# A graph-transformer layer: the linear attention's projections moved out of the sorting stage into the gather stage

## Chip, core and metric

The kernel runs on one core of a Trainium2 chip. A core has a matrix engine (TensorE, PE in the profile), a vector engine (VectorE, DVE), a scalar engine for activation functions (ScalarE, ACT), a general engine (GpSimd, POOL) and a sequencer that issues transfers (SyncE, SP). They run side by side and wait for each other by semaphores. [...] The metric is device time in microseconds of one execution, lower is better.

## What is computed

One layer of a graph transformer over 6,250 nodes with 256 features and 206,250 directed edges. Three parts, added up: graph attention over the edges, linear attention over all nodes, and a mixture of eight experts, of which two are chosen per node.

```
xn = layernorm(x)                                  # 6250 x 256
# graph attention: per edge (i <- j), 4 heads
p = xn @ W; e = exp(leaky_relu(p_i . Wl + p_j . Wr))
gnn_i = elu(sum_j e_ij * p_j / sum_j e_ij + b)
# linear attention, 4 heads of 32
q, k, v = split(rmsnorm(xn, g_pre) @ w_qkv)        # 128 columns each
k, v = concat(memory columns, k), concat(memory columns, v)
q = softmax over a head's 32 columns, times 32**-0.5
k = softmax over all nodes
context = k.T @ v                                  # per head, 32 x 32
mix = rmsnorm(q @ context @ w_out + b_out, g_out) + xn
x = x + gnn + mix
x = x + moe(layernorm(x)[None])                    # 8 experts, gelu, top 2
```

The softmax of k runs over all nodes, so its sum and its maximum for each of the 128 columns are only known when every node has been seen; q needs the context and so comes after.

## The kernel before

The nodes are cut into 49 tiles of 128 (the last has 106 rows), in 13 groups of up to four. The kernel has two stages of unlike work and a tail.

**The first stage** sorts the edges and makes the table from which they are gathered. The edges lie in 51 batches of 32 columns. `sort_batch` (L370) handles one: VectorE marks each edge's bucket (`ob`, L387), TensorE counts them (`n_ps`, L395), VectorE scans the counts (`inc`, L399) and spreads them (`ahead`, L412), TensorE forms ranks (`r_ps`, L419 and L420), VectorE takes their maximum (`rank`, L427), ScalarE converts it (`rank2`, L439), VectorE builds the payload (`rv`, two at L444) and the one-hot places (`ohp`, L448), TensorE puts the payload in place (`g_ps`, L454) and ScalarE stores it in `grid` (L459). The tiles `ob`, `inc`, `rank2`, `rv` and `ohp` have two buffers, `r_ps`, `n_ps` and `g_ps` one.

Between the batches `project` (L303) takes one group of nodes for every three batches: statistics on ScalarE, the normalized rows `xn` (L338), two transposes (L343), their copy `xT` (L345), and one product with a joined weight `wcat` (L348) whose 456 columns hold q, k, v (384) and what the graph part needs (72). ScalarE copies q to `q_all` (L351), k and v to `kv` (L352) and the rest to `tab` (L355), which goes to the table in memory. The scale of the rmsnorm, `rn`, is made per group by VectorE (L325 to L328), and the gain `g_pre` is multiplied into the weights once (L291).

When the last group is done, `context` (L467) runs between the remaining twelve batches: VectorE takes the maximum of k over all nodes (L468), GpSimd subtracts it (L498), ScalarE takes the exponential (L499), and TensorE adds up 49 products of k and v in one PSUM region (L502). The result, normalized and multiplied with `w_out`, is `cw` (L521).

**The gather stage** goes through the 49 tiles. `pack` (L875) prepares the edge lists of two tiles, in seven steps of products (`s_ps`, L940) with VectorE's operands (L923, L930, L935). `gather` (L969) lets GpSimd issue 35 indirect transfers per tile into `xe` (L972); `xe` has three buffers. `look` (L980) finds the destination terms (`oh` L984, transposes L997, `ohT` L1001, `e_ps` L1009), `weights` (L1016) makes the edge weights, and `sums` (L1035) adds up the weighted rows in four parts per tile (`ohw` L1041, `a_ps` L1048). A buffer of `xe` comes free when the tile's products at L1048 are done.

Beside the tiles runs a list of other work, `todo` (L1056), from which `some_more` (L1058) takes steps, each at a cost: a call takes up to two units (FC is 2), and a tile has four calls. First on it is `attention` (L574), three steps per group, priced at 2 each: softmax of q (L583 to L588); per tile a transpose, a product with `cw` (L598) and a square sum (L601); the normalization, with x read again (L609), added and written to `base_y` (L620). Its first VectorE operations are held behind the first finished pack by `later` (L567). When it is used up, the experts' weights are loaded and `finish_steps` (L661) of the finished blocks follows: products at L775 and L791, activation at L783, the sum at L795.

**The tail** finishes the experts of the last blocks.

The order on each engine is set by a scheduler at build time; each engine then runs its own list strictly in order. The prices at L1056 fix between which tiles a step stands.

Of the kernel before, what the change touches and what calls it, by code (L numbers as in the profile page):

```python
# [1 line left out]

# [6 lines left out]
F32 = mybir.dt.float32  # L9
F16 = mybir.dt.float16  # L10
BF16 = mybir.dt.bfloat16
I32 = mybir.dt.int32
AF = mybir.ActivationFunctionType
OP = mybir.AluOpType
# [3 lines left out]
P = 128  # L18
# [17 lines left out]
def tile_gps_layer(  # L36
# [53 lines left out]
    KW = 2 * HID + 1  # L90
    O_TAB = 3 * HID
    O_EL = O_TAB + H + FO
    PW = O_EL + H
    assert NPAD > N and PW <= 512 and last > 0
# [141 lines left out]
    with tc.tile_pool(name="ids", bufs=1) as lp:  # L236
# [21 lines left out]
    nc.scalar.dma_start(out=wcat[:, :, :3 * HID], in_=w_qkv.rearrange("(c p) f -> p c f", p=P))  # L258
    nc.scalar.dma_start(
        out=wcat[:, :, O_TAB + H:O_EL], in_=gnn_W.rearrange("(c p) f -> p c f", p=P)  # L260
    )
# [3 lines left out]
    gpre = kp.tile([P, DC], F32, name="gpre")  # L265
# [5 lines left out]
    wo = kp.tile([P, D], F32, name="wo")  # L271
    nc.scalar.dma_start(out=wo, in_=w_out)
    mk = kp.tile([P, NM], F32, name="mk")
    nc.scalar.dma_start(out=mk, in_=mem_kv[0].rearrange("h d m -> (h d) m"))
    mv = kp.tile([P, NM], F32, name="mv")
# [6 lines left out]
    for c in range(DC):  # L282
        wt_ps = mps.tile([FO, P], F32, name="tp")
        nc.tensor.transpose(wt_ps, wcat[:, c, O_TAB + H:O_EL], ident)
        wT = qw.tile([FO, P], F32, name="wT")
        nc.scalar.copy(wT, wt_ps)
        wlr_ps = mps.tile([P, 2 * H], F32, name="pr")
        nc.tensor.matmul(wlr_ps, lhsT=wT, rhs=lrT, start=True, stop=True)
        nc.scalar.copy(wcat[:, c, O_TAB:O_TAB + H], wlr_ps[:, :H])
        nc.scalar.copy(wcat[:, c, O_EL:PW], wlr_ps[:, H:])  # L290
        nc.vector.tensor_scalar(  # L291
            wcat[:, c, :3 * HID], wcat[:, c, :3 * HID], gpre[:, c:c + 1], None, op0=OP.mult
        )

    q_all = qp.tile([P, NT, HID], F32, name="q_all")
    kv = kp.tile([P, NT, KW], F32, name="kv")
    nc.gpsimd.memset(kv[:, :, KW - 1:KW], 1.0)
    kmax = kp.tile([P, HID], F32, name="kmax")

    def xn_of():  # L300
        return qw.tile([P, D], F32, name="xn")

    def project(t0, n):  # L303
# [10 lines left out]
        for j in range(n):  # L314
# [8 lines left out]
        rn = qw.tile([P, GT], F32, name="rn")  # L323
        nc.scalar.activation(rn[:, :n], var, AF.Sqrt, scale=float(D))
        nc.vector.tensor_mul(rn[:, :n], rn[:, :n], rs)  # L325
        nc.vector.tensor_scalar_max(rn[:, :n], rn[:, :n], 1e-12)
        nc.vector.reciprocal(rn[:, :n], rn[:, :n])
        nc.vector.tensor_scalar_mul(rn[:, :n], rn[:, :n], float(D) ** 0.5)  # L328
        shift = qw.tile([P, GT], F32, name="shift")
        nc.vector.scalar_tensor_tensor(  # L330
            shift[:, :n], stats[:, t0:t0 + n, 0], -1.0, rs, op0=OP.mult, op1=OP.mult
# [3 lines left out]
        for j in range(n):  # L335
            t = t0 + j
            xn = xn_of()
            nc.scalar.activation(  # L338
                xn, xt[:, j, :], AF.Identity, bias=shift[:, j:j + 1], scale=rstd[:, t:t + 1]
            )  # L340
            xT_ps = mps.tile([P, DC, P], F32, name="tp")
            for c in range(DC):
                nc.tensor.transpose(xT_ps[:, c, :], xn[:, c * P:(c + 1) * P], ident)  # L343
            xT = qw.tile([P, DC, P], F32, name="xT")
            nc.scalar.copy(xT, xT_ps)  # L345
            pr = mps.tile([P, PW], F32, name="pr")
            for c in range(DC):
                nc.tensor.matmul(  # L348
                    pr, lhsT=xT[:, c, :], rhs=wcat[:, c, :], start=(c == 0), stop=(c == DC - 1)
                )  # L350
            nc.scalar.activation(q_all[:, t, :], pr[:, :HID], AF.Copy, scale=rn[:, j:j + 1])  # L351
            nc.scalar.activation(  # L352
                kv[:, t, :2 * HID], pr[:, HID:3 * HID], AF.Copy, scale=rn[:, j:j + 1]
            )
            nc.scalar.copy(tab[:, j, :], pr[:, O_TAB:PW])  # L355
# [10 lines left out]
    def flat(t):  # L366
        return t.rearrange("p a b -> p (a b)")


    def sort_batch(t):  # L370
# [44 lines left out]
        r_ps = sps.tile([P, BW // BB, 512], F32, name="r_ps")  # L415
# [26 lines left out]
        rv = sw.tile([P, BW, 2, NB], F16, name="rv")  # L442
# [4 lines left out]
        ohp = sw.tile([P, BW, P], F16, name="ohp")  # L447
# [17 lines left out]


    def context():  # L467
        nc.vector.tensor_reduce(  # L468
            kmax, kv[:, :NT - 1, :HID].rearrange("p t d -> p d t"), axis=AX.X, op=OP.max
        )  # L470
        nc.vector.tensor_max(kmax[:last], kmax[:last], kv[:last, NT - 1, :HID])
        km_ps = mps.tile([HID, P], F32, name="tp")
        nc.tensor.transpose(km_ps, kmax, ident)
        kcol = kp.tile([P, 2], F32, name="kcol")
        nc.vector.tensor_reduce(kcol[:, 0:1], km_ps, axis=AX.X, op=OP.max)
        nc.vector.tensor_reduce(kcol[:, 1:2], mk, axis=AX.X, op=OP.max)
        kmc = kp.tile([P, 1], F32, name="kmc")
        nc.vector.tensor_max(kmc, kcol[:, 0:1], kcol[:, 1:2])
        kr_ps = mps.tile([P, HID], F32, name="tp")
        nc.tensor.transpose(kr_ps, kmc.to_broadcast([P, P]), ident)  # L480
        krow = kp.tile([P, HID], F32, name="krow")
        nc.vector.tensor_copy(krow, kr_ps)
        nkm = kp.tile([P, 1], F32, name="nkm")
        nc.vector.tensor_scalar_mul(nkm, kmc, -1.0)
        emk = kp.tile([P, NM], F32, name="emk")
        nc.scalar.activation(emk, mk, AF.Exp, bias=nkm)
        mm_ps = mps.tile([NM, 2, P], F32, name="tp")
        nc.tensor.transpose(mm_ps[:, 0, :], emk, ident)
        nc.tensor.transpose(mm_ps[:, 1, :], mv, ident)
        memT = kp.tile([NM, 2, P + 1], F32, name="memT")  # L490
        nc.vector.memset(memT, 1.0)
        nc.vector.tensor_copy(memT[:, :, :P], mm_ps)
        ctx_ps = mps.tile([P, HID + 1], F32, name="pr")
        nc.tensor.matmul(ctx_ps, lhsT=memT[:, 0, :P], rhs=memT[:, 1, :], start=True, stop=False)
        yield
        for t0, n in groups:
            kk = kv[:, t0:t0 + n, :HID]
            nc.gpsimd.tensor_sub(kk, kk, krow[:, None, :].to_broadcast([P, n, HID]))  # L498
            nc.scalar.activation(kk, kk, AF.Exp)  # L499
            for t in range(t0, t0 + n):  # L500
                rows = P if t < NT - 1 else last
                nc.tensor.matmul(  # L502
                    ctx_ps, lhsT=kv[:rows, t, :HID], rhs=kv[:rows, t, HID:KW],
                    start=False, stop=(t == NT - 1),
                )
            yield
        rden = kp.tile([P, 1], F32, name="rden")
        nc.vector.reciprocal(rden, ctx_ps[:, HID:HID + 1])
        nc.vector.tensor_scalar_mul(rden, rden, float(DH) ** -0.5)
        cbd = kp.tile([P, HID], F32, name="cbd")  # L510
        nc.vector.memset(cbd, 0.0)
        for h in range(MH):
            s = slice(h * DH, (h + 1) * DH)
            nc.vector.tensor_scalar(cbd[s, s], ctx_ps[s, s], rden[s], None, op0=OP.mult)
        cT_ps = mps.tile([P, HID], F32, name="tp")
        nc.tensor.transpose(cT_ps, cbd, ident)
        cT = kp.tile([P, HID], F32, name="cT")
        nc.scalar.copy(cT, cT_ps)
        cw_ps = mps.tile([P, D], F32, name="pr")
        nc.tensor.matmul(cw_ps, lhsT=cT, rhs=wo, start=True, stop=True)  # L520
        nc.scalar.copy(cw, cw_ps)  # L521
        yield
# [21 lines left out]
    steps = context()  # L544
    while batches:
        sort_batch(batches.pop(0))
        next(steps, None)
    for _ in steps:
        pass
# [17 lines left out]
    def later(ins):  # L567

        tc.add_manual_dep(
            ins.ins, gate[0].ins.name,  # L570
            mybir.DependencyInfo(mybir.DependencyClass.NoSync, mybir.DependencyReason.DATA),
        )

    def attention():  # L574
# [4 lines left out]
        for t0, n in groups:  # L579
# [10 lines left out]
            o_g = qw.tile([P, GT, D], F32, name="o_g")  # L590
            ss = qw.tile([P, GT], F32, name="ss")
            for j in range(n):
                qT_ps = yps.tile([P, P], F32, name="y_ps")
                nc.tensor.transpose(qT_ps, q_all[:, t0 + j, :], ident)
                qT = qw.tile([P, P], F32, name="qT")
                nc.scalar.copy(qT, qT_ps)
                o_ps = yps.tile([P, D], F32, name="y_ps")
                nc.tensor.matmul(o_ps, lhsT=qT, rhs=cw, start=True, stop=True)  # L598
                nc.vector.tensor_add(o_g[:, j, :], o_ps, brow)
                sq = qw.tile([P, D], F32, name="sq")  # L600
                nc.scalar.activation(sq, o_g[:, j, :], AF.Square, accum_out=ss[:, j:j + 1])  # L601
# [454 lines left out]
    todo = [(attention(), [FC] * (3 * len(groups)))]  # L1056
# [207 lines left out]
```

## Time and profile before

| | us |
|---|---|
| median of 3 runs (lowest, highest) | 4222.5 (4214.7, 4229.85) |
| the profiled execution | 4182.5 |
| its span, first to last instruction | 4180.7 |
| TensorE busy in the span | 2268.6 (54%) |
| VectorE busy | 1919.8 (46%) |
| GpSimd busy | 1669.8 (40%) |
| ScalarE busy | 746.2 (18%) |
| first gather starts | 446.2 |
| last gather ends | 3994.5 |

Busy time is the time in which an engine works on at least one instruction; a matrix engine's instructions overlap and their ends are modelled. `PEld` is the load of a stationary operand, which runs beside the products. The clock that the throttle granted to TensorE is given as a share of full speed. A wait is put down to whoever released it, by semaphore events; "remote" stands where the profile knows no releaser. The profiled execution was shorter than the median run, by 40 us.

### The profile page before, as it was taken

The numbers are of one execution on the slowest core, as the hardware profiler recorded it, in microseconds if no ns is written. First come the engines' busy times: TensorE is split into PE (matmuls) and PEld (weight loads), VectorE is DVE, ScalarE is ACT, GpSimd is POOL, SyncE is SP. The second block draws the span as 40 slices with busy tenths as digits, with TensorE's granted clock in tenths as the row PEclk, the third lists the DMA queues.
The fourth block names the chain that finished last, engine by engine and source line by source line (L and its number), as shares of the span: only waits on it lengthen the run. The fifth ranks groups of instructions, "written<-read, shape, count | busy, mean of one in ns | idle before, by whom it ended". The sixth has DMA issues, their size and how long they took to land. (4 is left out here: it accounts for less than half of the span.)

```text
span 4180.7 us, 39357 instructions
## 1 busy us (share of the span) xinstructions
PE 2268.6 (54%) x15401; PEld 1663.9 (40%) x15401; DVE 1919.8 (46%) x3941; ACT 746.2 (18%) x1653; POOL 1669.8 (40%) x1774
## 2 busy tenths in 40 slices
PE   7877232435254764644765555455364573554677
PEld 4544232324242543433543433334253352442456
DVE  7787444536352443533442523425343452342423
ACT  5542001212111111111111110111111111110122
POOL 1001545454445344344344344544535335344410
PEclk8875555666666877776877776777676686776778
DMA  1020111111121111011011100101101001011100
GB/s 59 28 29 1 21 28 41 37 41 37 34 74 20 22 19 23 18 24 22 12 29 18 25 17 17 30 17 22 25 12 27 18 19 25 13 25 19 23 12 7
DMA packets 106548, 103.75 MB, mean 25 GB/s; under 512 B 42678, under 2 KB 78740, under 8 KB 106356
## 3 DMA queue, kind: packets, MB, share of 16 engines
q0 software_dynamic: 54720, 60.52, 8.4%
q1 hardware_dynamic: 49940, 39.75, 3.3%
q8 instruction: 123, 2.02, 0.2%
q10 hardware_dynamic: 1696, 0.89, 0.1%
q14 instruction: 69, 0.57, 0.0%
HBM read 86.39 MB, written 14.65 MB: 24 GB/s over the span
## 5 line engine op out<-in xcount | busy, mean ns | idle before, releaser
L972 POOL DMA_INDIRECT xe<-table,dst_x x1710 | 1635.7, 957 | 2011.0 <-PE a_ps L1048 1323.2
L1048 PE MATMUL a_ps<-ohw,xe 128*65 128x128 f32 x4400 | 665.1, 307 | 235.7 <-issue 189.3
L1048 PEld LDWEIGHTS a_ps<-ohw,xe 128*65 128x65 f32 x4400 | 590.8, 159 | 314.4 <-issue 243.1
L775 PE MATMUL h_ps<-tokT,w1s 128*128 128x512 f32 (+3 forms) x896 | 442.8, 610 | 235.1 <-ACT hT L783 205.1
L795 DVE SCALAR_TENSOR_TENSOR x<-y_ps,comb,x 128x256 f32<-128x256 f32 x392 | 187.0, 481 | 782.4 <-remote 479.1
L791 PE MATMUL y_ps<-w2s,hT 128*128 128x256 f32 x1568 | 436.7, 413 | 147.6 <-issue 107.2
L791 PEld LDWEIGHTS y_ps<-w2s,hT 128*128 128x128 f32 x1568 | 315.5, 208 | 273.0 <-issue 177.5
L940 PE MATMUL s_ps<-rc,ohp 128*128 128x144 f16 x2525 | 255.1, 260 | 279.5 <-DVE ohp L935 146.8
L1041 DVE TENSOR_TENSOR ohw<-oh,bank 128x1280 f32<-128x1280 bf16 x196 | 321.5, 1641 | 170.1 <-remote 149.3
L940 PEld LDWEIGHTS <-ohp 128*128 128x128 f16 x2525 | 209.6, 114 | 324.2 <-DVE ohp L935 162.9
L1009 PE MATMUL e_ps<-elw,ohT 128*128 128x48 bf16 x588 | 36.2, 199 | 544.7 <-ACT ohT L1001 477.8
L783 ACT ACTIVATE hT<-h_ps,b1s 128x512 f32<-128x512 f32 (+3 forms) x224 | 140.4, 627 | 1018.4 <-remote 531.0
L775 PEld LDWEIGHTS h_ps<-tokT,w1s 128*128 128x128 f32 x896 | 171.8, 214 | 345.7 <-ACT hT L783 226.0
L1001 ACT COPY ohT<-t_ps 128x768 bf16<-128x768 bf16 x98 | 78.3, 799 | 1130.1 <-remote 842.3
L930 DVE TENSOR_TENSOR rc<-ohc,bank 128x1152 f16<-128x1152 f16 (+1 forms) x350 | 231.2, 687 | 64.8 <-remote 62.2
L1009 PEld LDWEIGHTS <-ohT 128*128 128x128 bf16 x588 | 27.0, 106 | 577.2 <-ACT ohT L1001 505.9
L935 DVE TENSOR_TENSOR ohp<-to,bank 128x2048 f16<-128x2048 f16 (+1 forms) x175 | 193.5, 1105 | 0.0
L763 PE MATMUL y_ps<-b2s,cTs 8*128 8x256 f32 x98 | 49.7, 600 | 192.4 <-ACT cTs L761 118.6
L764 DVE TENSOR_TENSOR x<-x,y_ps 128x256 f32<-128x256 f32 x49 | 20.6, 420 | 269.7 <-remote 164.6
L1018 DVE TENSOR_REDUCE z<-e_ps 128x140 f32<-128x420 f32 (+1 forms) x49 | 28.7, 585 | 244.6 <-PE e_ps L1009 224.1
L923 DVE TENSOR_TENSOR ohc<-to,bank 128x1152 f16<-128x1152 f16 (+1 forms) x175 | 119.6, 683 | 0.3 <-ACT to L911 0.2
L448 DVE TENSOR_TENSOR ohp<-rank,iota_h 128x4096 f16<-128x4096 f16 (+1 forms) x51 | 116.1, 2277 | 6.3 <-ACT rank L439 6.0
(273 smaller groups left out, 2568.0 us busy)
## 6 DMA issues: line engine op xcount, KB each, us to landing
xe<-table,dst_x POOLq DMA_INDIRECT x1710
xt<-in_x_dram SPq DMA_DIRECT2D x24, 512.0 KB
base_y<-xt SPq DMA_DIRECT2D x12, 512.0 KB
yt<-base_y SPq DMA_DIRECT2D x9, 512.0 KB
out_dram<-x SPq DMA_DIRECT2D x9, 512.0 KB
w1s<-in_L_ffn_w_dram SPq DMA_DIRECT2D x8, 256.0 KB
w2s<-in_L_ffn_w_dram SPq DMA_DIRECT2D x8, 256.0 KB
table<-tab SPq DMA_DIRECT2D x12, 138.0 KB
```

Source lines behind the costliest of these rows:

```text
L448: nc.vector.tensor_tensor(pairs(ohp[:, :w]), two(rank2[:, :w], P // 2), row(iota_h, P // 2), op=OP.is_equal)
L775: nc.tensor.matmul(h_ps[:, :w], lhsT=w1s[:, e, c, f * P:(f + 1) * P], rhs=held["tokT"][:, c, :w], start=(c == 0), stop=(c == DC - 1),)
L783: nc.scalar.activation(held[e][:, f, :w], h_ps[:, :w], AF.Gelu, bias=b1s[:, k:k + 1])
L791: nc.tensor.matmul(y_ps, lhsT=held[e][:, f, j * P:(j + 1) * P], rhs=w2s[:, e, f, :], start=(f == 0), stop=(f == FC - 1),)
L795: results.append(nc.vector.scalar_tensor_tensor(x2[:, j, :], y_ps, held["comb"][:, j, e:e + 1], x2[:, j, :], op0=OP.mult, op1=OP.add,))
L923: nc.vector.tensor_tensor(pairs(ohc[:, :m]), twos(to[:, 0, t0:t0 + m], U * CW // 2), iota_2[:, :, :U * CW // 2].to_broadcast([P, m, U * CW ...
L930: nc.vector.tensor_tensor(pairs(rc[:, :m, i, :]), pairs(ohc[:, :m]), twos(edges_q[:, t0:t0 + m, i, :], U * CW // 2), op=OP.mult,)
L935: nc.vector.tensor_tensor(pairs(ohp[:, :m]), twos(to[:, 1, t0:t0 + m], P // 2), iota_2.to_broadcast([P, m, P // 2, 2]), op=OP.is_equal,)
L940: nc.tensor.matmul(flat(s_ps), lhsT=ohp[:, t - t0, :], rhs=flat(rc[:, t - t0]), start=(t == 0), stop=(t == NBT - 1),)
L972: nc.gpsimd.indirect_dma_start(out=xe[:, c, :], out_offset=None, in_=table, in_offset=bass.IndirectOffsetOnAxis(ap=dst_x[:, c:c + 1], axis=0),
L1041: nc.vector.tensor_tensor(ohw[:, :n], oh[:, g0:g1, i, None, :].to_broadcast([P, n, H, SN]), ew_s[:, c0:c0 + n, :, None].to_broadcast([P, n ...
L1048: nc.tensor.matmul(a_ps[:, i].rearrange("f h n -> f (h n)"), lhsT=xe[:, c, H:], rhs=ohw[:, c - c0].rearrange("p h n -> p (h n)"), start=(c ...
```

## The change

Three things are changed.

1. `project` multiplies only with the 72 columns of the graph part; q, k and v leave the first stage, and with them `kv`, the scale per group and `context` in its old form. What the normalization needs later is kept for all tiles (`rn_all`, `shift_all`).
2. A new `context` stands at the head of the list `todo`, ahead of `attention`. It reads x a second time, normalizes it with the rmsnorm's scale, transposes it (into `xnT`), computes k transposed for a whole group in one product of up to 512 columns, keeps a running maximum over the groups and shrinks the old sums when it grows, computes q and v per tile, transposes the exponentials back and adds the group's product of k and v to `sums_c` on VectorE. It has three steps per group and two more; all steps of the list are now priced at 1 (80 of them; before 39 at 2), so that a call takes two.
3. In `sort_batch`, `r_ps` gets two PSUM regions and `rv` and `ohp` three buffers.

Some tiles of `attention` (`o_g`, `sq`) go from two buffers to one, and the small weights move to the pool that lives as long as the attention.

```diff
     wcat = kp.tile([P, DC, PW], F32, name="wcat")
-    nc.scalar.dma_start(out=wcat[:, :, :3 * HID], in_=w_qkv.rearrange("(c p) f -> p c f", p=P))
...
+    wqvk = qp.tile([P, DC, 3, HID], F32, name="wqvk")
+    for i, k in enumerate((0, 2, 1)):
+        nc.scalar.dma_start(
+            out=wqvk[:, :, i],
+            in_=w_qkv[:, k * HID:(k + 1) * HID].rearrange("(c p) f -> p c f", p=P),
+        )
...
-        rn = qw.tile([P, GT], F32, name="rn")
-        nc.scalar.activation(rn[:, :n], var, AF.Sqrt, scale=float(D))
-        nc.vector.tensor_mul(rn[:, :n], rn[:, :n], rs)
-        nc.vector.tensor_scalar_max(rn[:, :n], rn[:, :n], 1e-12)
-        nc.vector.reciprocal(rn[:, :n], rn[:, :n])
-        nc.vector.tensor_scalar_mul(rn[:, :n], rn[:, :n], float(D) ** 0.5)
+        nc.scalar.activation(rn_all[:, t0:t0 + n], var, AF.Sqrt, scale=float(D))
...
-            nc.scalar.activation(q_all[:, t, :], pr[:, :HID], AF.Copy, scale=rn[:, j:j + 1])
-            nc.scalar.activation(
-                kv[:, t, :2 * HID], pr[:, HID:3 * HID], AF.Copy, scale=rn[:, j:j + 1]
-            )
-            nc.scalar.copy(tab[:, j, :], pr[:, O_TAB:PW])
+            nc.scalar.copy(tab[:, j, :], pr)
...
-        r_ps = sps.tile([P, BW // BB, 512], F32, name="r_ps")
+        r_ps = sps.tile([P, BW // BB, 512], F32, name="r_ps", bufs=2)
...
-        rv = sw.tile([P, BW, 2, NB], F16, name="rv")
+        rv = sw.tile([P, BW, 2, NB], F16, name="rv", bufs=3)
...
-        ohp = sw.tile([P, BW, P], F16, name="ohp")
+        ohp = sw.tile([P, BW, P], F16, name="ohp", bufs=3)
...
-    steps = context()
     while batches:
         sort_batch(batches.pop(0))
-        next(steps, None)
-    for _ in steps:
-        pass
...
+    def context():
...
+        later(nc.vector.tensor_mul(rn_all, rn_all, rstd))
...
+        xt = load(0)
+        yield
+        for g, (t0, n) in enumerate(groups):
+            v = vs[g % 2]
+            xnT = qw.tile([P, DC, GT * P], F32, name="xnT", bufs=1)
+            for j in range(n):
+                t = t0 + j
+                xn = xn_of()
+                nc.scalar.activation(
+                    xn, xt[:, j, :], AF.Identity, bias=shift_all[:, t:t + 1],
+                    scale=rn_all[:, t:t + 1],
+                )
+                xT_ps = yps.tile([P, DC, P], F32, name="y_ps")
+                for c in range(DC):
+                    nc.tensor.transpose(xT_ps[:, c, :], xn[:, c * P:(c + 1) * P], ident)
+                nc.scalar.copy(xnT[:, :, j * P:(j + 1) * P], xT_ps)
+            if g + 1 < len(groups):
+                xt = load(g + 1)
+            yield
+            w = (n - 1) * P + rows_of(t0 + n - 1)
+            k_ps = hps.tile([P, GT * P], F32, name="h_ps")
+            for c in range(DC):
+                nc.tensor.matmul(
+                    k_ps[:, :w], lhsT=wqvk[:, c, 2], rhs=xnT[:, c, :w],
+                    start=(c == 0), stop=(c == DC - 1),
+                )
+            here = small("here")
+            nc.vector.tensor_reduce(here, k_ps[:, :w], axis=AX.X, op=OP.max)
+            new = small("most")
+            nc.vector.tensor_max(new, most, here)
+            less = small("less")
+            nc.vector.tensor_scalar_mul(less, new, -1.0)
+            shrink = small("shrink")
+            nc.scalar.activation(shrink, most, AF.Exp, bias=less)
+            most = new
+            ekT = qw.tile([P, GT * P], F32, name="ekT", bufs=1)
+            nc.scalar.activation(ekT[:, :w], k_ps[:, :w], AF.Exp, bias=less)
+            for j in range(n):
+                qv_ps = yps.tile([P, 2, HID], F32, name="y_ps")
+                for c in range(DC):
+                    nc.tensor.matmul(
+                        flat(qv_ps), lhsT=xnT[:, c, j * P:(j + 1) * P],
+                        rhs=flat(wqvk[:, c, :2]), start=(c == 0), stop=(c == DC - 1),
+                    )
+                nc.scalar.copy(q_all[:, t0 + j, :], qv_ps[:, 0])
+                nc.scalar.copy(v[:, j, :HID], qv_ps[:, 1])
+            yield
+            ek_ps = yps.tile([P, GT, P], F32, name="y_ps")
+            ek = qw.tile([P, GT, P], F32, name="ek", bufs=1)
+            for j in range(n):
+                r = rows_of(t0 + j)
+                nc.tensor.transpose(ek_ps[:r, j, :], ekT[:, j * P:j * P + r], ident)
...
+            nc.scalar.copy(ek[:r, :n], ek_ps[:r, :n])
+            c_ps = yps.tile([P, HID + 1], F32, name="y_ps")
+            for j in range(n):
+                nc.tensor.matmul(
+                    c_ps, lhsT=ek[:r, j, :], rhs=v[:r, j, :], start=(j == 0), stop=(j == n - 1)
+                )
+            nc.vector.scalar_tensor_tensor(
+                sums_c, sums_c, shrink, c_ps, op0=OP.mult, op1=OP.add
+            )
+            yield
...
-    todo = [(attention(), [FC] * (3 * len(groups)))]
+    todo = [(chain(context(), attention()), [1] * (6 * len(groups) + 2))]
```

## The prediction

> **What bounds the kernel now.** I read the slices first, then the stretches that they suggested, then the waits inside each, and the timeline of two tiles. The page:
>
> ```profile
> PE   7877232435254764644765555455364573554677
> DVE  7787444536352443533442523425343452342423
> POOL 1001545454445344344344344544535335344410
> PEclk8875555666666877776877776777676686776778
> ```
>
> One digit is 104.5 us of the span of 4180.7. Up to slice 4 TensorE and VectorE are busy and GpSimd is not: the first stage. From there to slice 38 GpSimd gathers and nobody is full. The stretches (us, then busy time and count per engine, granted clock, DMA share, GB/s):
>
> ```profile
> 40.00:287.00 247.00, 219.72 (x2583) 129.90 (x2583) 191.45 (x312) 145.89 (x565) 4.56 (x24) 0.81 0.11 32
> 287.00:412.00 125.00, 82.44 (x1123) 57.88 (x1122) 103.12 (x128) 25.91 (x86) 19.32 (x15) 0.60 0.12 2
> 412.00:446.00 34.00, 16.08 (x107) 12.14 (x107) 31.20 (x72) 0.89 (x4) 0.00 (x0) 0.50 0.00 1
> 446.00:1306.00 860.00, 328.01 (x2214) 267.37 (x2215) 403.07 (x843) 122.29 (x272) 440.93 (x455) 0.63 0.17 39
> 1306.00:3994.00 2688.00, 1459.25 (x8470) 1067.76 (x8468) 1096.77 (x2351) 381.20 (x569) 1194.29 (x1255) 0.72 0.11 21
> ```
>
> Sorting with projections (40 to 287) is held by TensorE, 219.7 of 247; the rest of the sort (287 to 412) by VectorE, 103.1 of 125. Then the first pack (34 us), then the gathers. Their waits, between 500 and 1250, and VectorE's between 40 and 290:
>
> ```profile
> POOL xe L972 <- PE a_ps L1048: 178.5, 8, 26.0
> ```
>
> ```profile
> DVE rv L444 <- PE g_ps L454: 39.6, 28, 4.6
> DVE ob L387 <- PE r_ps L419: 9.8, 9, 1.1
> DVE rank L427 <- PE r_ps L420: 3.7, 6, 1.4
> ```
>
> Each tile issues 35 gathers, 1.25 us apart (44 us, "the burst"); then GpSimd waits some 25 us until the sums that read its oldest buffer are done. How the other engines use burst and gap shows in two attention stretches and two expert ones:
>
> ```profile
> 1099.00:1142.70 43.70, 6.74 (x58) 5.53 (x57) 18.78 (x36) 5.10 (x16) 33.33 (x35) 0.65 0.18 40
> 1142.70:1168.40 25.70, 17.43 (x148) 15.78 (x148) 12.54 (x18) 7.77 (x17) 0.00 (x0) 0.74 0.03 3
> 1967.40:2018.80 51.40, 45.90 (x232) 32.99 (x233) 24.17 (x66) 11.17 (x19) 0.03 (x1) 0.82 0.02 1
> 2018.80:2062.30 43.50, 21.30 (x92) 12.73 (x90) 13.99 (x21) 1.72 (x3) 33.09 (x35) 0.67 0.15 28
> ```
>
> In a burst TensorE gets through 53 to 116 matmuls (mean 83 over 44 bursts), whether much waits or little; then all three compute engines stand still, mostly until its end. The rest of a tile's stream runs in the gap. So the gap is as long as the stream: a straight line (least squares) through the 44 periods from the third burst on, each with the matmul count of its stretch, gives 35.9 us + 0.167 us per matmul (residual 4.8 us). Tiles with 280 to 290 matmuls took 80 to 95 us, those with about 205 took 63 to 66. (An fp32 product that is no transpose counts as two matmuls in the trace, and here.) That line is my price for work added there.
>
> **The change, part by part.**
>
> *Projection in the first stage.* The matmuls of L348 go from 456 columns to 72. Their group is 196 rows, 109.8 us busy. The nearest narrow row, L712 (8 columns, also 196), is 35.6; I take 45, so TensorE loses some 65 us, 60 of them between 40 and 287: 219.7 to 160. ScalarE loses L351 and L352 (17.8 + 22.9), VectorE four tiny operations per group (L325 to L328, 13 x 4 x 0.14 = 7 us). VectorE, 191.5 - 6 = 185 us there, is now the longer engine. The fewer matmuls also let the clock sag: it was 0.81 there and 0.60 between 287 and 412, where sort matmuls cost 3.9 us a batch (82.4 less 18.1 for L502 and 2 small, over 16 batches). 34 batches at that rate plus the remaining 22 + 45 us of transposes and projections come to 200, so TensorE is close behind and the section can't fall much under 200: -30 to -50, taken -35.
>
> *More buffers.* Two regions for the rank sums and three payload and place tiles go at exactly the 39.6 + 9.8 + 3.7 us above. They are what lets VectorE fill its stretch; I don't count them twice. If they did nothing, VectorE keeps its 77% of the section: 185/0.775 = 239, a gain of 8.
>
> *Context out of the first stage.* L468 (11.0 us on VectorE) and some 4 us of small operations go, with 49 matmul pairs (L502, 18.1 us) and GpSimd's L498 (19.0, hidden). VectorE has 88 us left of 125; at its present 82% fill 107, at 90% with the buffers 98: -18 to -27, taken -20. On the start: the load that the first transpose waits for comes earlier and ScalarE issues two more DMAs (it waits 8.8 us for ten), +-2, taken 0. First stage in all -55. The ends: -26 (no help from buffers, 8 + 18) and -82 (VectorE 95% full, 88/0.95 = 93 and so 32, with the 50 that TensorE allows).
>
> *Context in the gather stage.* Per group of four tiles: 8 transposes, 4 matmuls of 512 columns, 16 of 256, 4 transposes, 8 of 129: 40 rows, 12.25 groups, about 497 with the few single ones. In the built instruction order they stand in tiles 0 to 4, 85 to 110 each, where before there were 12 to 24 of attention; attention's 147 stand in tiles 5 to 9, 24 to 36 each instead of 12. At 0.167 us each 497 cost +83. From above: in the ten gaps after the bursts 2 to 11 TensorE did 1043 matmuls in 245 us, 4.25 per us, so 497/4.25 = +117. From below: if the five bursts took 116, the most seen, instead of 83, that hides 165 matmuls or 27 us, and VectorE is relieved in those tiles of some 8 us each (12 of attention against 4 of context), at 0.38 us of gap per us of VectorE (a second line through the gaps: 6.8 + 0.73 of TensorE's busy time + 0.38 of VectorE's) 15 us: +40. ScalarE adds 4 x 0.606 (as L338) + 4 x 0.385 (L345) + 8 x 0.265 (L596) + 0.2 + 0.63 (L585) + 0.58 (L1106) = 7.5 us a group, 18 us a tile, where it has some 10 of 70; it hides in the gap as long as the matmul stream is longer, and if it ran serially with TensorE it adds up to half of its 92 us. VectorE adds 1.5 us a group (a 512-element maximum, L583 0.68, and small ones), which hides under attention's work that left these tiles; in tiles 5 to 9 it has attention twice as dense, +17 instructions a tile, about 8 us beside a gap of 30. The line prices matmuls alone, so I leave that in the range.
>
> *DMAs and queues.* SP loads x a second time for the context: 12 x 512 KB + 106 KB, ahead of attention's loads and of the writes of base_y, with the two xt buffers shared. ScalarE now waits for each load in xn; behind it stand the copies of ohT, for which TensorE's e_ps already waits 160.5 us between 500 and 1250, and through them the sums and GpSimd. Loads are asked for a group ahead, and before no row waited for an x load in attention: 0, from above 13 x 5.1 us (the one wait for xt, at the start) = 66. GpSimd's gathers themselves are untouched: 35 per tile before and after. The ScalarE table loads of Sqrt and Exp are fewer (no alternation in tiles 0 to 4), 1.28 us each, hidden.
>
> Gather stage +85 (the line's 83 and 2 for the rest), ends +40 and +130 (117 and a part of ScalarE's time). Sum: -55 + 85 = **+30**. The profiled execution took 4182.5 (span 4180.7, 1.8 around it), so it would take 4212; the runs have a median of 4222.5, 40 above the profiled one, and I add the 30 there: **4252 us**.
>
> The granted clock is 0.81 where the work leaves and 0.63 where it arrives. [...]
>
> **Rivals.**
> 1. *The holes take it* (faster). Bursts leave TensorE idle for over 30 of 44 us; if the context runs there, the gather stage pays 20 and the net is -35: 4188. For: the engine is only 38% busy between 446 and 1306 (328 of 860), and the first burst of 70 gathers waits for nothing but the second pack. Against: expert tiles had work ready and still did 53 to 102 in a burst. It decides from a price under 0.11 us per moved matmul (55/497). Chance 0.21.
> 2. *The first stage does not give* (the change doesn't do what it says there): VectorE goes on waiting for ranks through ScalarE, -26 instead of -55: 4281. For: half of its waits come from TensorE's order, not its load. Against: 39.6 us of them sit on one buffer that is tripled. Chance 0.15.
> 3. *ScalarE becomes the path in tiles 0 to 4*: transposes, copies, exponentials and x loads in series, gather +130: 4297. For: it starts under 17 instructions in a burst and now has 38 to 56 a tile. Chance 0.12.
>
> **How the numbers follow.** The forecast, with its own range 4230 to 4275, gets 0.52. Nothing here can be told from no change within 0.3%, 12.7 us. Rival 1 holds most of faster (0.17 of it, the rest of it within 0.3%); the low edge of the forecast adds 0.02 and, within 0.3%, 0.09: faster 0.19, same 0.13, slower 0.68. For 8 in 10 the range goes from 4190 (first stage -82, gather +50) to 4298 (rival 3).
>
> **What would show it.** First gather at 385 to 400 us instead of 446, fewer waits of rv for g_ps, VectorE over 85% in the first stage; tiles 0 to 4 with periods near 82 us where 559 to 820 had a mean of 65 (261.5/4), tiles 5 to 9 near 72, the rest as before to a few us. It is wrong if tiles 0 to 4 stay under 72 (rival 1), if the first gather comes after 420 (rival 2), or if ScalarE's waits for x loads appear among the long ones (rival 3).

## The result and the profile after

| | before | after |
|---|---|---|
| median, us (4 runs each) | 4220.18 (4214.70 to 4229.85) | 4258.92 (4255.45 to 4262.35) |
| ratio, 95% interval | | 1.0094 [1.0072, 1.0116] |
| profiled execution, us | 4182.5 | 4256.38 |
| first gather, us from the span's start | 446.2 | 422.1 |
| first gather to eleventh burst | 722.2 | 771.0 |
| eleventh burst to the end of the span | 3012.3 | 3061.5 |

The change costs 39 us here; 30 were forecast. The profiled execution after lies 2.5 us under its median, the one before 38 under, so 35 of the 74 us between the two spans are no work of the change. I put them in the last stretch, whose work it hardly touches (9,661 matmuls instead of 9,631). What the change did is in the two stretches ahead: 24 us won up to the first gather, 49 lost from there to the eleventh burst. Both are about half of what I had worked out. They add up to 25 us; the other 14 of the 39 would lie in the last stretch, and no run explains them.

The page's slices after (one digit 106 us):

```profile
PE   6776245645443666574655554455364473554677
DVE  6778244435554353443443433524334353343423
POOL 1000553444545334335354344444535335344410
PEclk8555577766666777686877776777677686776787
```

The last row is the first surprise: where it had 8 and 7 in the first stage it now has 5. The same stretches as before (us, then busy time and count of PE, PEld, DVE, ACT, POOL, then granted clock, DMA share, GB/s), and the eleven bursts:

```profile
40.00:287.00 247.00, 194.52 (x2438) 139.72 (x2437) 176.13 (x247) 112.05 (x456) 5.01 (x22) 0.60 0.10 29
287.00:412.00 125.00, 82.49 (x1192) 52.95 (x1190) 113.23 (x179) 18.95 (x79) 0.29 (x2) 0.50 0.13 7
...
422.10:1193.10 771.00, 360.52 (x2297) 284.76 (x2297) 336.55 (x709) 150.27 (x426) 369.75 (x386) 0.67 0.19 37
```

Between 40 and 287 TensorE lost 25 us of busy time, not the 60 of the freed columns, and VectorE is busy for 176 instead of 191: 71%, not over 85%. Its waits there (who waits for whom, us in total, times, longest):

```profile
DVE rank L416 <- PE r_ps L409: 44.2, 12, 4.7
DVE ohp L437 <- ACT rank L428: 13.8, 13, 1.2
DVE ob L376 <- PE r_ps L408: 10.5, 10, 2.1
```

The wait of rv for g_ps, 39.6 us before, is gone as the buffers promised. In its place stand waits for the ranks: these three lines make 68.5 us, the three before 53.1.

In the gather stage GpSimd waits for the sums as before, longer, and a burst and the gap after it look like this:

```profile
POOL xe L1023 <- PE a_ps L1099: 223.9, 8, 34.6
```

```profile
677.00:721.40 44.40, 12.60 (x86) 9.50 (x84) 18.40 (x36) 6.25 (x19) 34.02 (x35) 0.70 0.20 34
721.40:756.00 34.60, 29.43 (x217) 24.82 (x218) 21.12 (x36) 13.93 (x40) 0.01 (x1) 0.84 0.13 33
```

The burst took 86 matmuls, about as many as before; the gap took 217, with TensorE busy for 29.4 of 34.6 us. Nearly all that was added ran in the gaps. Over the second to sixth burst TensorE did 452 matmuls (430 before), in the gaps after them 870 (494), and these gaps grew from 110 to 150 us. In the next five the gaps took 627 instead of 516 and grew by 8 us. 487 matmuls more in the gaps for 48 us: 0.10 us each. The gaps had room for some of them: TensorE was busy for 69 of the 110 us, and is for 122 of the 150, so 53 us more of its work cost 40 us of time. That this is why they were cheap is read from these counts; no run leaves the context out of a gather stage like this one.

### The profile page after: what moved, and what is told of

It reads as the page before. It is cut to its first block, busy times and chain, and to the rows that moved or that the text cites. A ratio compares the mean times of both kernels' runs of the same rounds, so it can differ in the third digit from the quotient of the medians.

```text
span 4254.6 us, 40336 instructions
## 1 busy us (share of the span) xinstructions
PE 2349.0 (55%) x15794; PEld 1741.4 (41%) x15794; DVE 1912.1 (45%) x3946; ACT 763.9 (18%) x1763; POOL 1646.5 (39%) x1760
## 5 line engine op out<-in xcount | busy, mean ns | idle before, releaser
L1099 PE MATMUL a_ps<-ohw,xe 128*65 128x128 f32 x4400 | 641.8, 301 | 167.6 <-issue 95.5
L1099 PEld LDWEIGHTS a_ps<-ohw,xe 128*65 128x65 f32 x4400 | 574.5, 156 | 231.8 <-issue 127.1
L437 DVE TENSOR_TENSOR ohp<-rank,iota_h 128x4096 f16<-128x4096 f16 (+1 forms) x51 | 115.0, 2254 | 14.0 <-ACT rank L428 13.8
```

Source lines behind the costliest of these rows:

```text
L437: nc.vector.tensor_tensor(pairs(ohp[:, :w]), two(rank2[:, :w], P // 2), row(iota_h, P // 2), op=OP.is_equal)
L1099: nc.tensor.matmul(a_ps[:, i].rearrange("f h n -> f (h n)"), lhsT=xe[:, c, H:], rhs=ohw[:, c - c0].rearrange("p h n -> p (h n)"), start=(c ...
```

## The same change with another bound

The parts were to be priced by leaving each out. The first four such kernels ran on one chip (number 10) together with the kernel before, and there that kernel took 2738 us instead of 4220. So both kernels were run again as they are, on chip 12:

> The changed kernel itself, beside the kernel before on one chip. In the first runs of experiments the kernel before took 2738 us instead of 4220, with its gathers back to back from the first to the last, and every kernel's time was its first gather + 2296 us. If that law holds here too: first gather at 420 to 430, total 2716 to 2726, 0.4 to 0.8% faster than the kernel before, and nothing is paid in the gather stage. If the chip stands still in the bursts as in the first pair of profiles: total near 4259 against 4220, ratio 1.007 to 1.012.

> The kernel before, for its profile beside the others. If the gathers run back to back: first gather at 442 (2738 less 2296), VectorE's waits in the first stage as in the first profile (rv for g_ps about 40 us), the granted clock near 0.8 between 40 and 287. If the engines stand still in the bursts: first gather at 446 and total near 4220.

| chip 12 | before | after |
|---|---|---|
| median, us | 2739.54 | 2715.93 |
| ratio, 95% interval | | 0.9910 [0.9896, 0.9925] |
| first gather | 444.8 | 421.7 |
| rest (profiled run less first gather) | 2294 | 2297 |

Here the same change is 0.9% faster. Its first stage is what it was, to half a microsecond in the first gather; the gather stage is another one. Busy tenths of TensorE and GpSimd, first of the kernel before on chip 12:

```profile
PE   6888664375555399989699869498596799796887
...
POOL 1000113777777777777777777777777777777710
```

and of the changed kernel there, with two stretches of its gather stage:

```profile
PE   5777754698576589898897979497694899786877
...
POOL 1000006777777777777777777777777777777710
```

```profile
446.00:1306.00 860.00, 664.07 (x4584) 521.66 (x4585) 653.35 (x1402) 262.95 (x607) 654.91 (x674) 0.87 0.29 58
1306.00:2600.00 1294.00, 1045.65 (x6778) 806.21 (x6777) 870.86 (x1888) 308.49 (x465) 974.60 (x1018) 0.87 0.22 35
```

GpSimd's gathers follow each other without a hole, 674 in 860 us, one in 1.27 us, and 1710 of them are the 2167 and 2169 us that the two kernels spend there. Nothing waits for the end of a burst (GpSimd's waits for `a_ps` between 500 and 1250 us come to 0.3 us, against 223.9 above): TensorE does 4584 matmuls in these 860 us, where the changed kernel's first profile has 2297 in 771. Beside that stream the context is free (2297 us from the first gather on, against 2294).

What differs shows in a few lines. TensorE in a burst of the changed kernel in its first profile (start, duration, engine, line, what, count, idle time before it):

```profile
2091.05 0.58 PE L842 MATMUL y_ps<-w2s,hT 128*128 128x256 f32 x1 [2.22 <-issue]
2093.85 0.58 PE L842 MATMUL y_ps<-w2s,hT 128*128 128x256 f32 x1 [2.21 <-issue]
2096.64 0.59 PE L842 MATMUL y_ps<-w2s,hT 128*128 128x256 f32 x1 [2.21 <-issue]
```

and the kernel before on chip 12 while gathers are issued:

```profile
1299.72 1.89 PE L791 MATMUL y_ps<-w2s,hT 128*128 128x256 f32 x8
1301.45 2.78 PE L1048 MATMUL a_ps<-ohw,xe 128*65 128x128 f32 x24
1304.07 1.89 PE L791 MATMUL y_ps<-w2s,hT 128*128 128x256 f32 x8
```

One matmul in 2.80 us, waiting for nothing but its own issue, against eight of the same line in 1.89. In the first pair, whose record names no chip, the engines are held back while gathers are issued; on chips 4, 10 and 12 they are not. Whether that is the chip or its condition at the time, and what holds the engines, isn't settled. Slower transfers are not it: those of the gathers kept the 16 DMA engines busy for 9.9% of 4254.6 us in the first profile of the changed kernel and for 15.6% of 2716.5 on chip 12, some 420 us in both. One lead: the first trace of the changed kernel holds 6,207 records of transfers that landed, the one of chip 12 holds 29,289, with 1710 gathers in both. Whether the missing records and the held engines belong together, no run here tests, and no later run met the held condition again.

All runs below are from chips 4, 10 and 12, where the kernel before took 2738.0 to 2740.7 us. There the profiled time less the first gather is 2291 to 2299 us in every kernel, so they measure the first stage, and price the gather stage at nothing. The prices of the held gather stage rest on the first pair of profiles alone. Each ratio below is to the kernel before on the same chip, taken beside it; the first gather is that of the one profiled execution.

| kernel | median, us | ratio to before, 95% interval | first gather |
|---|---|---|---|
| before | 2739.54 | | 444.8 |
| after | 2715.93 | 0.9910 [0.9896, 0.9925] | 421.7 |
| after, context left out | 2725.56 | 0.9952 [0.9938, 0.9966] | 430.0 |
| after, wide projection kept | 2715.85 | 0.9912 [0.9899, 0.9926] | 419.5 |
| after, old buffers | 2716.43 | 0.9924 [0.9910, 0.9938] | 420.0 |
| after, wide projection, old buffers | 2716.42 | 0.9904 [0.9889, 0.9919] | 424.1 |
| before, new buffers | 2756.65 | 1.0066 [1.0052, 1.0080] | 461.0 |
| before, narrow projection | 2745.48 | 1.0025 [1.0016, 1.0034] | 450.3 |
| before, context left out | 2707.69 | 0.9895 [0.9881, 0.9909] | 415.8 |
| after, projection spread | 2717.85 | 0.9924 [0.9910, 0.9937] | 420.6 |
| before's first stage, context moved | 2713.27 | 0.9898 [0.9885, 0.9911] | 415.0 |
| same, 200 columns | 2711.44 | 0.9910 [0.9888, 0.9932] | 410.3 |

## The experiments

**What the moved work costs.** The context is left out of the gather stage, and its results are zeros:

```diff
...
-    todo = [(chain(context(), attention()), [1] * (6 * len(groups) + 2))]
+    todo = [(attention(), [FC] * (3 * len(groups)))]
```

> The changed kernel without the context: the second projection of x, the key maximum, the exponentials and the sums over nodes are left out of the gather stage (queries and context are zeros), so the output is not the reference's. It prices the 497 moved matmuls. By my line (0.167 us each) the first eleven bursts take 771 - 83 = 688 us and the total is near 4175. By what the two traces show so far (bursts 0 to 10: 722 before, 771 after, so 0.1 us each): 715 to 730 us, total near 4210. If the holes take them (rival 1): over 750 us, total over 4235.

All three numbers were meant for a gather stage that is held in its bursts; the kernel met the free one. First gather 430.0 (a memset of the queries' tile, put in for the zeros, delayed the start: the first payload `rv` began at 29.9 us instead of 23.0), then 2296 to the end, as with the context: here the 497 matmuls cost nothing. What they cost in a held gather stage stays untested.

**The width of the projection.** The 384 columns are put back into the first stage, unused:

```diff
...
-            pr = mps.tile([P, PW], F32, name="pr")
+            pr = mps.tile([P, PW + 3 * HID], F32, name="pr")
...
```

> The changed kernel with the 384 columns of queries, keys and values projected again in the first stage, the result unused (the context is still computed in the gather stage). Clock theory (the freed columns let TensorE's granted clock fall from 0.81 to 0.60 between 40 and 287 us, so the matmuls that stayed became dearer and nothing was won): the clock comes back to about 0.8 there, the rank sums of 416 columns cost 0.37 us each instead of 0.51 and 0.49, and the first gather comes no later than the 422.1 of the changed kernel, more likely near 405, although TensorE has some 50 us more to do; total 4240 to 4260. Load theory (TensorE's work sets the stage and the clock follows other things): the first gather comes 25 to 35 us later, at 445 to 460, total near 4290.

First gather 419.5 against 421.7, the total as far under the kernel before as the changed kernel's own: 52 us more of products (100.0 us from 40 to 287 instead of 47.9) cost nothing. Groups between 40 and 287 (line, engine, shape, count, busy us, mean ns, idle before), of the changed kernel in its first profile and of this one:

```profile
L443 PE MATMUL g_ps<-rv,ohp 128*128 128x52 f16 x1056 | 52.0, 222 | 28.4 <-DVE ohp L437 28.4
...
L408 PE MATMUL r_ps<-ob,upto_own 128*128 128x416 f16 x63 | 32.0, 511 | 0.0
...
L336 PE MATMUL tp<-ident,xn 128*128 128x128 f32 x88 | 28.0, 422 | 0.0
```

```profile
L444 PE MATMUL g_ps<-rv,ohp 128*128 128x52 f16 x1056 | 41.1, 198 | 17.7 <-DVE ohp L438 17.7
...
L409 PE MATMUL r_ps<-ob,upto_own 128*128 128x416 f16 x65 | 26.1, 402 | 1.6 <-DVE rank L417 1.6
L337 PE MATMUL tp<-ident,xn 128*128 128x128 f32 x88 | 22.2, 342 | 0.0
```

With the wide product in between, these matmuls are shorter: rank sums 402 ns instead of 511, transposes 342 instead of 422, placements 198 instead of 222. (The counts into `n_ps` are not: 164 ns in both.) The same holds in every run here: with a product of 456 columns between them the rank sums of that row take 374 to 416 ns, with 200 columns 449, with 72 columns 510 to 528. The clock theory holds as far as "no later"; the 405 that I thought likelier didn't come. The other way round, narrowing in the kernel before, where ScalarE's copies of q, k and v go with it and constants stand in for them:

```diff
...
-                    pr, lhsT=xT[:, c, :], rhs=wcat[:, c, :], start=(c == 0), stop=(c == DC - 1)
+                    pr, lhsT=xT[:, c, :], rhs=wcat[:, c, O_TAB:], start=(c == 0), stop=(c == DC - 1)
...
```

> The kernel before with the projection of 72 columns and without ScalarE's copies (queries, keys and values are constants, so the output is not the reference's); the context stays in the first stage, old buffers. My prediction's step (projection alone -35): first gather at 405 to 415, total near 2704. Clock theory (the freed columns are given back by dearer matmuls): 440 to 450, total within 0.3% of the kernel before, rank sums at 0.50 us or more instead of 0.37.

First gather 450.3, total 0.25% slower (some of that may be GpSimd's memsets of the constants; the first payload began 4 us later). Rank sums took 520 ns. So 384 columns fewer gave nothing, in both directions.

One thing stands beside all these comparisons: the order of each engine's instructions is fixed when the kernel is built, and a changed part brings another order. TensorE's sequence of products before the first gather is the same in both traces of the kernel before (3943 matmuls in each) and in both of the changed kernel (3836), and another one with the other width or the other buffers. So each price here is that of a part together with its new order.

**The buffers.** Taken out of the changed kernel, and put alone into the kernel before (`bufs=2` for r_ps, `bufs=3` for rv and ohp):

> The changed kernel with one region for the rank sums and two payload and place tiles, as before. If the buffers are what lets VectorE fill its stretch (my prediction's step): rv waits for g_ps again, 40 us or more in the first stage, the first gather at 445 to 460 instead of 422, total near 4290. If the clock holds the stage whatever the buffers (clock theory): first gather at 422 to 432, total within 0.3% of the changed kernel. If the buffers did harm (they let TensorE run ahead and the ranks come later): the first gather comes before 415.

> The kernel before with two regions for the rank sums and three payload and place tiles, nothing else. Clock theory: the wide projection keeps the clock at 0.8, VectorE loses its 39.6 + 9.8 us of waits in part, the first gather comes at 415 to 430 instead of 446, and the total is 15 to 30 us under the kernel before (4190 to 4205). Rival (the buffers change only where VectorE waits): first gather 440 to 450, total within 0.3%.

Out of the changed kernel: first gather 420.0, no difference, although `rv` waited for `g_ps` again, for 18.5 us from 40 to 287. Put alone into the kernel before: 461.0, the total 18 us longer, which neither theory had. VectorE's longest waits there, 40 to 287:

```profile
DVE ob L387 <- PE r_ps L419: 44.2, 21, 4.4
DVE rank L427 <- PE r_ps L420: 19.1, 9, 2.2
```

`rv` no longer waits, but in the new order it is `ob` and `rank` that meet rank sums which TensorE hasn't done: 53 us of waits in three lines became 63 in these two. Whether the buffers in the old order would have gained was not tried.

**The context out of the first stage.** First with the wide projection and the old buffers both back in the changed kernel, then by itself in the kernel before:

```diff
...
-    steps = context()
     while batches:
         sort_batch(batches.pop(0))
-        next(steps, None)
...
```

> The changed kernel with both the wide projection in the first stage (384 columns whose result is unused) and the old buffers: of the change's first-stage parts only the context moved out is left. If the moved context alone gives what the first stage gains, and narrowing and buffers nothing: first gather at 400 to 420, no later than the 419.5 of the wide projection with new buffers. If the narrow projection is what gives the gain: 430 or later. The total by the law above 2296 us more.

> The kernel before with its context left out (no key maximum, no exponentials of keys, no sums over nodes; the context is zero, so the output is not the reference's); projection of 456 columns, ScalarE's copies of queries, keys and values and the old buffers stay. If the context between the last sixteen batches is all that the first stage gains: first gather at 420 to 425 instead of 444.8, total 2714 to 2720. If ScalarE's two copies per tile, which every kernel with the moved context also lost, are part of it: first gather at 430 to 440, total 2725 to 2735.

First gathers 424.1 and 415.8. The first lies between the two outcomes forecast for it, in the slowest of that kernel's six executions (2721.65, median 2716.42), so it decides nothing. The second is earlier than either forecast: 30.6 us in the median, more than the whole change. It is also the cleanest of these runs, since the order on TensorE is that of the kernel before up to 287 us and VectorE's waits there are the same (`rv` 39.8 us, `ob` 9.8). The whole first stage, from the start to the first gather, of the kernel before on chip 12, of this one, and of the changed kernel on chip 12:

```profile
0.00:444.80 444.80, 334.24 (x3943) 207.66 (x3943) 349.75 (x564) 190.61 (x716) 34.01 (x64) 0.74 0.13 28
0.00:415.80 415.80, 317.49 (x3836) 192.23 (x3836) 329.85 (x548) 181.11 (x699) 15.18 (x52) 0.74 0.14 30
0.00:421.70 421.70, 300.41 (x3836) 208.47 (x3836) 321.62 (x495) 149.33 (x601) 15.76 (x51) 0.68 0.13 29
```

VectorE (the third busy time) works longest in all three, here for 330 us instead of 350. Of the 29 us gained, 20 are work that left it and 9 are time in which it stood (95 us before, 86 here). The changed kernel takes 28 us of work off VectorE, 8 more than the context alone, mostly the scale per group; it gains 23, since VectorE stands for 100 us there. So the work that left VectorE accounts for the gain of the first stage, and 5 us of it are lost again in longer waits. ScalarE's copies, the rival, are not needed for it: this kernel keeps them and has the lowest median of all.

**The order on TensorE.** What is left between 40 and 287 looked like one wait of 4.7 us in each group, for rank sums that stand behind three tiles of the next projection. The projection was spread between the batches and held behind the rank sums ahead of it:

```diff
...
-        project(t0, n)
-        for _ in range(3):
+        parts = project(t0, n)
+        next(parts)
+        for k in range(3):
+            next(parts, None)
             sort_batch(batches.pop(0))
+        for _ in parts:
+            pass
```

> The changed kernel with the projection's four tiles spread between the sort batches: a tile's transposes may not stand in TensorE's order before the rank sums of the batch ahead of it. Order theory (what is left of the first stage's loss is one wait of 4.7 us in each of 12 groups, in which VectorE waits for rank sums that stand in TensorE's order behind three tiles of projection): the long waits of rank for r_ps go, 44.7 us in 40 to 287 become 10 to 20, first gather at 385 to 405, total 2680 to 2700. Clock theory alone (TensorE at half rate is simply too slow, in whatever order): first gather at 415 to 430, total 2710 to 2725.

The order theory falls. The long waits did go, and the same time came back elsewhere:

```profile
DVE ohp L451 <- ACT rank L442: 23.9, 19, 2.2
DVE rank L430 <- PE r_ps L422: 20.9, 18, 2.4
DVE inc L401 <- PE n_ps L397: 12.2, 17, 1.6
DVE ob L389 <- PE r_ps L421: 7.4, 7, 1.5
```

64 us in four places instead of 68.5 in three, first gather 420.6. VectorE waits for a TensorE that is slower per matmul (528 ns per rank sum in this trace, 376 in the kernel before), wherever in the order it meets it; the clock recorded from 40 to 287 is 1.00, so the half rate of the other theory is not in this trace, only the dear matmuls are. That this is the whole of what is left is argued from the durations and not shown.

**A version for both.** If width and buffers give nothing and the context everything, the first stage should stay as it was, without its context; queries are kept from there and only keys and values projected again beside the gathers. A variant drops keys and values from the first projection (200 columns):

> A version meant to beat both: the first stage of the kernel before, unchanged in width, copies and buffers, only without its context; the context of the changed kernel in the gather stage, with queries kept from the first stage and only keys and values projected again there. Its first stage is that of the kernel before without context, whose gathers began at 415.8. If the moved context costs nothing in the gather stage: first gather at 415 to 420, total 2706 to 2713, about 0.3% under the changed kernel's 2715.9 and 1.0 to 1.2% under the kernel before. If something of the moved context is on the path there: over 2716.

> As the version before it, but keys and values are not projected in the first stage (200 columns instead of 456, no copy of keys and values). Clock theory (width gives nothing either way): first gather between 412 and 425, total 2706 to 2722, transposes and rank sums dearer than with 456 columns (0.34 and 0.37 us there). If width is worth what I forecast (35 us for 384 columns): first gather near 392, total near 2685.

2713.3 and 2711.4 us. The first gather of the first version came at 415.0, as in the kernel without context, so the context moved beside the gathers costs the first stage nothing. The median is 5.6 us above that kernel's, just over the forecast range, but the kernel before was slower beside it too (2740.7 against 2738.3), and the ratios, 0.9898 and 0.9895, are not apart. Both versions beat the kernel before by 0.9 to 1.0%. Against the changed kernel they are 2.7 and 4.5 us lower in the median, which the intervals don't separate. The narrower one has the earliest gather of all, 410.3, and dearer rank sums, 449 ns instead of 374; the 392 that my price per column would have given is excluded again. Neither ran in a held gather stage.

## Why the prediction was right, and where it wasn't

The time, the sign and the range held for the pair they were made for: 4252 forecast, 4258.9 measured. The steps did not all hold: the first stage gave 24 us instead of 55, the gather stage took 49 instead of 85, and that two errors of over 30 us cancelled is luck. The two measured terms make +25; the +39 of the medians has 14 us more that no term accounts for.

- *"Projection in the first stage ... taken -35"*: this step failed; measured 0 (wide against narrow after: 0.1 us) and +7 (before). I had expected the clock to sag and reckoned 200 us for the section from it (TensorE was busy for 194.5, not the 160 of the freed columns), but then took TensorE's shorter stream as VectorE's gain. The section has no single full engine (after the change TensorE is busy for 194.5 and VectorE for 176.1 of 247 us): rank sums go from TensorE to VectorE to ScalarE and back. When the wide product left, placements became 10% dearer (201 to 222 ns) and rank sums 36% (376 to 511 ns), and waits for the ranks took the place of the wait for `g_ps`. What makes them dearer is not shown: the recorded clock fell with TensorE's busy time in this pair (0.81 to 0.60, at 219.7 and 194.5 us), but in other runs it stands at 1.00 beside rank sums as dear (last section). I had set the first stage's clock of 0.81 beside the 0.63 of the gather stage; the dearer matmuls counted in the first stage itself, which loses the work.
- *"More buffers ... are what lets VectorE fill its stretch"*: failed. They removed the named wait, and others came up; alone, in the order that came with them, they cost 18 us, in the changed kernel they give nothing.
- *"Context out of the first stage ... taken -20"*: right in mechanism, too small: -29 alone. VectorE lost 20 us of work, not the 15 that I counted from L468 and "some 4 us of small operations", and stood 9 us less.
- *First stage in all -55*: -24 in the pair, -23 on chip 12. Rival 2, the first stage that does not give, had -26 and VectorE waiting for ranks; its mark, a first gather after 420, came true (422.1), with most of the waits on TensorE's rank sums (44.2 us) and fewer on ScalarE (13.8).
- *"At 0.167 us each 497 cost +83"*: the term was mis-sized: 49 us, 0.10 us each. The line through the periods was fitted mostly on expert tiles, in whose gaps TensorE was busy for 79% of the time before the change (661 of 833 us after the bursts 21 to 46); in the tiles 0 to 4 it was 63% (69 of 110 us), and the context raised that to 82%. My own end "from below", +40, was nearer, though not for its reason. The mechanism held: the second to sixth burst took 22 matmuls more and the gaps after them 376.
- *Tiles 0 to 4 near 82 us, 5 to 9 near 72* (a burst and the gap after it): 73.6 and 71.9, where they had 65.4 and 69.6. The first is the mis-sized price again, and only just above the 72 that I had named as the sign of rival 1.
- *The holes take it* (rival 1) would have decided below 0.11 us per matmul. The price did come out below; the time did not turn, since the 55 us on the other side weren't there. Where the engines run through the bursts this rival is the whole truth of the gather stage, at a price of 0, and the change is faster.
- *ScalarE becomes the path* (rival 3): `xn`, which reads the loaded x, is not among ScalarE's waits.

What no step had: that the standing still in the bursts, which I took from one profile as the nature of the kernel, is absent elsewhere.

## What to carry to other kernels

When an engine is relieved in a stage where several engines hand work round in a circle, price what the others wait for, not the engine's total: width, buffers and order each removed a named wait here, and the wait came back under another name, while what clearly shortened the stage was work taken off VectorE. A part that is added or removed also brings another instruction order, which alone can move such waits (68.5 us in three lines became 64 in four when only the order was changed); compare the order before a price is read from the time. A price per instruction fitted on one kind of tile should be fitted on the kind of work that is moved. And a cost that rests on engines standing still for no reason in the program should be measured a second time, on another chip: here it decided the sign.

## What was not expected of the hardware

- One program, one input: 4220 us in the first pair, 2738 to 2741 on chips 4, 10 and 12. The traces differ in whether TensorE, VectorE and ScalarE run on while GpSimd issues gathers; why is open.
- The granted clock does not always tell. In the changed kernel with old buffers it is recorded as 1.00 from 40 to 287, and the rank sums are as dear as anywhere:

```profile
40.00:287.00 247.00, 205.56 (x2506) 141.49 (x2505) 182.57 (x255) 115.39 (x461) 10.33 (x22) 1.00 0.10 30
```

```profile
L408 PE MATMUL r_ps<-ob,upto_own 128*128 128x416 f16 x65 | 34.3, 528 | 4.9 <-DVE rank L416 4.9
```

528 ns at a recorded 1.00, 511 at 0.60, 376 at 0.81; the narrow projection in the kernel before has 520 at 0.88, the changed kernel on chip 12 517 at 0.73. So the durations were taken as evidence and the clock as a hint.
- More work on TensorE can be free: 52 us of unused products left the ratio to the kernel before where it was (0.9912, against 0.9910 without them).
